# Four graph layers on one core: the R values of single edges picked two or three units ahead inside the products and summed one unit early, the spread of R moved there too, and the projection steps placed behind the products

## The chip, the core and the metric

The kernel runs on one core of one Trainium2 chip. The metric is the device time of one execution in microseconds (us): before the change the median of three runs is 2439.98 us (2439.79 to 2440.81). PE is the matrix engine (TensorE), PEld its weight loads, DVE the VectorE, ACT the ScalarE, POOL the GpSimd engine, SP the SyncE, which here only issues DMAs.

## The reference, cut to what matters

The input is x, 3327 rows of 512, and a 0/1 matrix adj of 3327 x 3327 whose rows and columns get sparser toward the end. Four layers follow one another, each on a layer-normed, clipped x and each added to x. Layers 0, 2 and 3 are graph attention with 8 heads of 64; layer 1 averages neighbours and multiplies.

```python
# attention (layer 2; 0 and 3 differ in names and in what follows)
Wh = jnp.einsum('nd,hdo->hno', x, W)
f1 = jnp.einsum('hno,ho->hn', Wh, a1)
f2 = jnp.einsum('hno,ho->hn', Wh, a2)
e = jax.nn.leaky_relu(f1[:, :, None] + f2[:, None, :], negative_slope=ALPHA)
e = jnp.where(adj[None, :, :] > 0, e, NEG_INF)
attention = jax.nn.softmax(e, axis=-1)
h_prime = jnp.einsum('hnm,hmo->hno', attention, Wh)
out = jax.nn.elu(h_prime)
...
h = jnp.maximum(_layernorm(x, axis=-1), 0.0)
x = x + _L2_gnn_ref(h, adj, L2_gnn_W, L2_gnn_a1, L2_gnn_a2)
```

Layer 0 puts a batch normalization and a relu after the product in place of the elu.

## The kernel before, in words

The program first makes, in the stretch up to about 352 us, lists of the neighbours of each group of 64 target rows (a group is `g`, 52 of them, two to a block of 128), and the projection of layer 0. Then it takes the sparse path, `sparse`; a dense path, `general`, is in the program but not run here.

One attention layer is one call of `attend` (L1319). The exponential of a leaky relu of a sum is written as a maximum of two products, so that a weight is max(R of the target, T of the source), times a factor of the source that is already inside the table's rows. R stands in `r_dram` and, as three bf16 parts whose sum is R, in `r3`; T and the projected values stand in a row of `table`.

The source rows of a group are cut into units (L1328). A *slot unit* holds up to 2 blocks (SLOTS) of 128 source rows with dense masks; a *unit of single edges* holds up to 3 (UNIT). There are 85 slot units and 90 units of single edges in a layer; most groups have one slot unit and then one or two units of single edges.

- A slot unit: `spread` (L1345) copies R of the group's 64 targets to all partitions with one product (L1350) into the bank `r_bc`. DVE takes the maximum with T (L1531, into the PSUM tile `mx`) and multiplies by the mask (L1535, `wgt`). PE multiplies the rows by it (L1564), 16 products a row (32 matmul records of the profile for two rows).
- A unit of single edges: each row belongs to one target. `pick` (L1470, product L1479) fetches its R by multiplying the transposed one-hot matrix `edges` with the three parts `r3`, into the PSUM tile `r_of`. DVE sums the three parts (L1517), takes the maximum with T (L1518), and scales the row (L1521, `vw`). PE adds it into its target with the one-hot matrix `ones_of` (L1553). `w_of`, the sum, lies in the PSUM tile of `mx`.
- In layer 0 alone the one-hot matrices are made on the way: DVE takes the bits (L1422), ACT makes masks of them (`masks`, L1439 to L1444), PE transposes them (`turned`, L1454), and ACT copies them to `edges` and out to `edges_dram` (`kept`, L1466). Layers 2 and 3 hold all `edges` in SBUF; layer 2 reads them back from `edges_dram` in five parts in its first five units (L1508).
- `load` (L1405) issues the fetches of a unit's rows three units ahead, from SP (contiguous rows) and POOL (gathers, L1314). `fetch` (L1339) loads R for the spread, two groups ahead.
- `later` (L1399) makes one step of each open `ending` (L1353: ACT copies the accumulator `facc` out, L1383, DVE takes reciprocals, L1387, ACT scales, L1393, then the layer's finish), and one of the work that goes beside the layer: in layer 0 the products and sums for layer 1 and for the batch normalization (`beside`, L1625; the sums L1675 and L1679), in layer 2 the projection for layer 3 (`Following.tick`, L841, with `norm`, L895, and `rest`, L960: p_ps L964, p_sd L972, p_wh L985, p_tr L999).

The order on PE, DVE and ACT is the order in which the code issues the work (L1336); semaphores are put in for the dependencies. PSUM tiles r_of, r_bc and mx have one buffer, the accumulator has two. For unit i the loop (L1503) issues: `load(i + 3)`; DVE's work of unit i, for single edges with the reduction L1517 first; `early(i)` (masks, then kept); `pick(i + 1)`; a spread for the next group if unit i-1 was the last slot unit; `later`; the next group's fetch; the products of unit i; and `turned`. `lead` (L1486) says how many units ahead the masks of a unit are made: 3 for single edges in layer 0, 2 in the others, 1 for slot units. `due(i)` lists the units whose turn it is.

Of the kernel before, what the change touches and what calls it, by code (L numbers as in the profile page):

```python
# [23 lines left out]
F32 = mybir.dt.float32  # L24
# [9 lines left out]
ALU = mybir.AluOpType  # L34
# [5 lines left out]
P = 128  # L40
H = 8
# [10 lines left out]
GB = 64  # L52
# [755 lines left out]
class Following:  # L808
# [468 lines left out]
def sparse(ctx: ExitStack, tc: tile.TileContext, t: dict, out: bass.AP, WA, ls, cs, idx, rdeg, first):  # L1277
# [41 lines left out]
    def attend(layer, table, r_dram, r3, finish, tick=lambda: None, home=None, beside=None, edges=None):  # L1319
# [14 lines left out]
        with tc.tile_pool(name=f"fatt{layer}", bufs=2) as ap, tc.tile_pool(  # L1334
            name=f"facc_ps{layer}", bufs=2, space=PSUM
        ) as aps, tc.manual_schedule(engines={ET.PE, ET.DVE, ET.Activation}):  # L1336
            loaded, ones_of, st_of, found, rrs, rbs, accs, ends, over = {}, {}, {}, {}, {}, {}, {}, [], []

            def fetch(j):  # L1339
                if j < len(groups):  # L1340
# [114 lines left out]

            def kept(i):

                if i < len(units) and units[i][2]:
                    _, g, _, rows, s0, _, _, _ = units[i]
                    u, n = g % PG, len(rows)  # L1460
                    mine = slice(u * GB, (u + 1) * GB)
                    if layer:
                        st_of[i] = edges[mine, s0 : s0 + n, :]
                        return
                    to = ap.tile([P, UNIT, P], BF16, name="edges", tag="edges", bufs=3)
                    nc.scalar.copy(to[mine, :n, :], st_of[i][mine, :n, :])  # L1466
                    nc.sync.dma_start(edges_dram[mine, s0 : s0 + n, :], to[mine, :n, :])
                    st_of[i] = to[mine, :n, :]

            def pick(i):  # L1470

                if i < len(units) and units[i][2]:
                    _, g, _, rows, s0, _, _, _ = units[i]
                    b, u = divmod(g, PG)
                    mine = slice(u * GB, (u + 1) * GB)
                    st = st_of.pop(i)
                    re = found[i] = aps.tile([P, UNIT, 3 * H], F32, name="r_of", tag="r_of", bufs=1)
                    for k in range(len(rows)):
                        nc.tensor.matmul(re[:, k, :], st[:, k, :], r3[mine, b, :], start=True, stop=True)  # L1479

            for j in range(2):
                fetch(j)
            spread(0)
            for i in range(AHEAD):
                load(i)
            lead = [(3 if layer == 0 else 2) if u[2] else 1 for u in units]  # L1486

            def due(i):

                return [k for k in range(max(i + 1, 0), i + 4) if k < len(units) and k - lead[k] == i]  # L1490
# [12 lines left out]
            for i, (j, g, e, rows, s0, begins, stops, last_slots) in enumerate(units):  # L1503
                n, m0 = len(rows), rows[0][0]
                gt = loaded.pop(i).bitcast(F32)
                T = gt[:, :n, H * (F + 1) : ROW]
                load(i + AHEAD)
                if layer == 2 and i < EPARTS:  # L1508
                    for u in range(PG):
                        mine = slice(u * GB, (u + 1) * GB)  # L1510
                        cut = slice(i * ls.used[u] // EPARTS, (i + 1) * ls.used[u] // EPARTS)
                        nc.sync.dma_start(edges[mine, cut, :], edges_dram[mine, cut, :])
                if e:
                    re = found.pop(i)
                    mx = aps.tile([P, SLOTS, H, GB], F32, name="w_of", tag="mx", bufs=1)
                    w = mx[:, 0, :UNIT, :H]
                    nc.vector.tensor_reduce(w[:, :n], re[:, :n].rearrange("p k (t h) -> p k h t", h=H), AX.X, ALU.add)  # L1517
# [3 lines left out]
                    nc.vector.tensor_tensor(  # L1521
                        vw[:, :n],
                        gt[:, :n, : H * (F + 1)].rearrange("p k (h x) -> p k h x", x=F + 1),
                        w[:, :n].unsqueeze(3).to_broadcast(full),
                        ALU.mult,
                    )
                else:
                    mk = mask[:, m0 : m0 + n, :]
                    full = [P, n, H, GB]
                    mx = aps.tile([P, SLOTS, H, GB], F32, name="mx", tag="mx", bufs=1)  # L1530
                    nc.vector.tensor_tensor(  # L1531
                        mx[:, :n], rbs[j].unsqueeze(1).to_broadcast(full), T.unsqueeze(3).to_broadcast(full), ALU.max
                    )
                    wt = ap.tile([P, SLOTS, H, GB], F32, name="wgt", tag="wgt", bufs=2 if layer == 0 else 3)
                    nc.vector.tensor_tensor(wt[:, :n], mx[:, :n], mk.unsqueeze(2).to_broadcast(full), ALU.mult)  # L1535
# [12 lines left out]
                for k in range(n):  # L1548
                    f, l = begins and k == 0, stops and k == n - 1
                    if e:  # L1550
                        by = vw[:, k].rearrange("p (q v) x -> p v q x", v=PG)
                        for v in range(PG):
                            nc.tensor.matmul(  # L1553
                                accs[g][v * GB : (v + 1) * GB, :sw].rearrange("p (q x) -> p q x", x=F + 1),
                                ones_of[i][:, k, :],
                                by[:, v],
                                start=f,
                                stop=l,
                            )
                        continue  # L1560
                    for q in range(hq):
                        for v in range(PG):
                            h = q * PG + v
                            nc.tensor.matmul(  # L1564
                                accs[g][v * GB : (v + 1) * GB, q * (F + 1) : (q + 1) * (F + 1)],
                                wt[:, k, h, :],
                                gt[:, k, h * (F + 1) : (h + 1) * (F + 1)],
                                start=(f and q == 0),
                                stop=(l and q == hq - 1),
                            )  # L1570
# [384 lines left out]
```

## Time and profile before

The profiled execution took 2678.83 us, the median of the runs 2439.98 us.

| What | Before |
|---|---|
| profiled execution, whole time | 2678.83 us |
| its span, first to last instruction | 2677.0 us |
| mean granted PE clock | 0.818 |
| lists and projection of layer 0 | 0 to about 352 us |
| attention of layer 0 | about 352 to 919 us |
| batch normalization, own part of layer 1 | about 919 to 1057 us |
| neighbours of layer 1, projection of layer 2 | about 1057 to 1517 us |
| attention of layer 2 | about 1552 to 2160 us |
| attention of layer 3 | about 2160 to 2660 us |

How to read it: a busy time is the union of an engine's instructions. A group of instructions has a line of the kernel, its count, its mean and the idle time of its engine just before it, with what ended that wait. A line "PE facc L1553 <- DVE vw L1521: 55.0, 48, 4.8" of the table of waits says that PE idled 55.0 us in 48 places, 4.8 at most, before products of L1553 until a DVE instruction of L1521 signalled. "issue" is idle time for which no semaphore is seen. Matmul ends are modelled[...].

### The profile page before, as it was taken

The page shows a single profiled execution, that of the slowest core. Times are in us where ns is not written, and L with a number is a line of the kernel's source. Part 1 is how long each engine was busy: PE and PEld are TensorE (multiplying, and loading weights), DVE is VectorE, ACT ScalarE, POOL GpSimd, SP SyncE. Part 2 cuts the span into 40 slices and gives each one's busy share as a digit, 9 for nine tenths or more (in the row PEclk, how much of TensorE's full clock was granted, in tenths as well). Part 3 has the DMA queues.
Part 4 walks back from the last instruction along what each step waited for, and adds up shares of the span by engine and source line. Part 5 has one row for each costly group of instructions (what it writes and reads, how often), then busy time and mean ns, then how long its engine had stood idle before and what let it go on. Part 6 is the DMA issues. An engine that isn't in the chain of part 4 may idle for free. (4 is left out here: it accounts for less than half of the span.)

```text
span 2677.0 us, 42990 instructions
## 1 busy us (share of the span) xinstructions
PE 1997.4 (75%) x14899; PEld 1129.0 (42%) x14899; DVE 1702.2 (64%) x3061; ACT 1113.8 (42%) x4149; POOL 1161.1 (43%) x1227
## 2 busy tenths in 40 slices
PE   6987157877777688879889847788788766767675
PEld 4644024545444344323333335454444444444442
DVE  5457856676667692124344557777667657788785
ACT  4555003344555542223233203667676702344443
POOL 1000034556655301666656245554445235666562
PEclk8788578988888899889999957889878866776676
DMA  7674068787777483778778587777667367887783
GB/s 278 237 269 172 7 226 273 241 254 213 220 219 234 131 292 129 259 239 266 249 234 274 161 259 221 210 229 210 203 187 217 104 212 224 233 242 237 223 248 94
DMA packets 213726, 577.60 MB, mean 216 GB/s; under 512 B 37838, under 2 KB 44076, under 8 KB 210174
## 3 DMA queue, kind: packets, MB, share of 16 engines
q0 software_dynamic: 93504, 328.25, 40.6%
q1 hardware_dynamic: 119998, 246.53, 27.6%
q8 instruction: 120, 1.97, 0.3%
q14 instruction: 104, 0.85, 0.1%
HBM read 511.41 MB, written 63.25 MB: 215 GB/s over the span
## 5 line engine op out<-in xcount | busy, mean ns | idle before, releaser
L1314 POOL DMA_INDIRECT rows_e<-table,idx x654 | 626.8, 958 | 395.4 <-issue 167.5
L1553 PE MATMUL facc<-vw,ones_of 128*64 128x260 f32 x2616 | 491.8, 496 | 101.9 <-DVE vw L1521 55.0
L1564 PE MATMUL facc<-rows_s,wgt 128*64 128x65 f32 x7200 | 353.7, 253 | 192.8 <-issue 117.4
L1564 PEld LDWEIGHTS facc<-rows_s,wgt 128*64 128x64 f32 x7200 | 305.7, 164 | 271.2 <-issue 166.7
L1314 POOL DMA_INDIRECT z_rows<-h_dram,idx x291 | 277.8, 955 | 301.9 <-issue 172.4
L1521 DVE TENSOR_TENSOR vw<-rows_e,w_of 128x1040 f32<-128x1040 f32 (+1 forms) x270 | 395.6, 1465 | 9.3
L1314 POOL DMA_INDIRECT rows_s<-table,idx x219 | 209.2, 955 | 418.0 <-PE r_of L1479 187.3
L1553 PEld LDWEIGHTS facc<-vw,ones_of 128*64 128x64 f32 x2616 | 236.5, 170 | 304.4 <-issue 193.2
L1531 DVE TENSOR_TENSOR mx<-r_bc,rows_s 128x1024 f32<-128x1024 f32 (+1 forms) x255 | 280.6, 1100 | 77.6 <-PE facc L1553 17.9
L1393 ACT ACTIVATE fhp<-sums,rd 64x64 f32<-64x64 f32 x816 | 215.5, 334 | 250.4 <-DVE rd L1387 199.6
L1535 DVE TENSOR_TENSOR wgt<-mx,mask 128x1024 f32<-128x1024 f32 (+1 forms) x255 | 280.3, 1099 | 50.5 <-PE facc L1564 24.2
L1517 DVE TENSOR_REDUCE w_of<-r_of 128x16 f32<-128x48 f32 (+1 forms) x270 | 60.7, 225 | 237.5 <-PE r_of L1479 103.5
L1839 PE MATMUL sage_acc<-z_rows,z_mask 128*64 128x512 f32 x736 | 189.0, 622 | 5.9 <-DMA z_rows<-h_dram 5.3
L1218 POOL DMA_DIRECT2D list_b<-shift x8 | 4.0, 514 | 322.2 <-DVE shift L1179 322.2
L1823 ACT CAST z_mask<-mask 128x128 f32<-128x128 uint8 (+1 forms) x201 | 52.0, 284 | 195.0 <-PE sage_acc L1839 85.2
L1792 DVE TENSOR_TENSOR s_o<-n_ps,bn_y 128x512 f32<-128x512 f32 x26 | 18.0, 692 | 173.6 <-PE n_ps L1787 105.0
L1383 ACT COPY sums<-facc 128x260 f32<-128x260 f32 x153 | 56.9, 372 | 164.8 <-PE facc L1553 116.3
L1444 ACT ACTIVATE mask<-on 128x128 uint8<-128x128 uint16 (+1 forms) x85 | 25.2, 296 | 240.9 <-DVE on L1422 199.7
L741 PE MATMUL wh_ps<-fWt,hT 128*128 128x512 f32 x208 | 122.2, 742 | 0.0
L1787 PE MATMUL n_ps<-fWx,aT 128*128 128x512 f32 x208 | 99.8, 624 | 20.4 <-issue 16.3
L926 PE MATMUL p_wh<-fWt,hT 128*128 128x512 f32 x208 | 104.0, 647 | 13.2 <-ACT hT L921 11.1
L1393 ACT ACTIVATE bn_y<-sums,rd 64x64 f32<-64x64 f32 x408 | 107.7, 334 | 3.1 <-DVE rd L1387 1.5
(260 smaller groups left out, 3038.3 us busy)
## 6 DMA issues: line engine op xcount, KB each, us to landing
adj_i<-in_adj SPq DMA_DIRECT2D x26, 1664.0 KB
rows_s<-table SPq DMA_DIRECT2D x46, 528.0 KB
table<-v_row SPq DMA_DIRECT2D x78, 264.0 KB
rows_s<-table SPq DMA_DIRECT2D x62, 264.0 KB
rows_s<-table SPq DMA_DIRECT2D x23, 632.0 KB
fin_x<-fx SPq DMA_DIRECT2D x52, 256.0 KB
z_rows<-h_dram SPq DMA_DIRECT2D x23, 512.0 KB
rows_e<-table,idx POOLq DMA_INDIRECT x654
```

The costliest lines, as they stand in the source:

```text
L741: nc.tensor.matmul(wh, hT[:, kc, :], self.Wt[:, kc, :], start=(kc == 0), stop=(kc == KC - 1))
L926: nc.tensor.matmul(wh, hT[:, kc, :], self.Wt[:, kc, :], start=(kc == 0), stop=(kc == KC - 1))
L1314: nc.gpsimd.indirect_dma_start(out=dst, out_offset=None, in_=src[:, :], in_offset=bass.IndirectOffsetOnAxis(ap=idx[:, k : k + 1], axis=0))
L1393: nc.scalar.mul(hp[o0 : o0 + GB, h * F : (h + 1) * F], sm[mine, q, 0:F], rd[mine, q, :])
L1517: nc.vector.tensor_reduce(w[:, :n], re[:, :n].rearrange("p k (t h) -> p k h t", h=H), AX.X, ALU.add)
L1521: nc.vector.tensor_tensor(vw[:, :n], gt[:, :n, : H * (F + 1)].rearrange("p k (h x) -> p k h x", x=F + 1), w[:, :n].unsqueeze(3).to_broadca ...
L1531: nc.vector.tensor_tensor(mx[:, :n], rbs[j].unsqueeze(1).to_broadcast(full), T.unsqueeze(3).to_broadcast(full), ALU.max)
L1535: nc.vector.tensor_tensor(wt[:, :n], mx[:, :n], mk.unsqueeze(2).to_broadcast(full), ALU.mult)
L1553: nc.tensor.matmul(accs[g][v * GB : (v + 1) * GB, :sw].rearrange("p (q x) -> p q x", x=F + 1), ones_of[i][:, k, :], by[:, v], start=f, stop=l,
L1564: nc.tensor.matmul(accs[g][v * GB : (v + 1) * GB, q * (F + 1) : (q + 1) * (F + 1)], wt[:, k, h, :], gt[:, k, h * (F + 1) : (h + 1) * (F + 1)],
L1787: nc.tensor.matmul(ps, aT[:, kc, :], Wx[:, 1, kc, :], start=(kc == 0), stop=(kc == KC - 1))
L1839: nc.tensor.matmul(acc[u * GB : (u + 1) * GB, :], m, z, start=f, stop=l)
```

## The change

For single edges, the pick of unit i+2 (layer 0) or i+3 (layers 2 and 3) is issued inside the products of unit i, after the products of its first row, or after all of them where the unit has one row (`others`). The spread for the next group goes there too, in the last slot unit itself. `r_of` keeps one buffer in layer 0 and gets two in the others. The reduction of unit i+1 (`summed`) is issued at the end of DVE's work of unit i. `later` comes after the products and the transposes. In `early`, kept copies come ahead of the masks. The five loads of edges in layer 2 come a unit earlier, the first ahead of the loop. `norm` yields once more between its ACT sums and the reciprocal square root on DVE. On each engine the number of instructions of each kind stays the same; of the projection of layer 3, four score products (L972) move from the loop to the stretch after it.

```diff
@@ norm
         step = rsqrt(nc, pp, cs, st[:, 2:3], 1.0 / D)
         yield
+        yield
         y = step()
@@ attend
-            loaded, ones_of, st_of, found, rrs, rbs, accs, ends, over = {}, {}, {}, {}, {}, {}, {}, [], []
+            loaded, ones_of, st_of, found, w_of, rrs, rbs, accs, ends, over = {}, {}, {}, {}, {}, {}, {}, {}, [], []
+            ahead = 2 if layer == 0 else 3
@@ kept
-                if i < len(units) and units[i][2]:
+                if layer == 0 and i < len(units) and units[i][2]:
...
-                    if layer:
-                        st_of[i] = edges[mine, s0 : s0 + n, :]
-                        return
@@ pick
-                    st = st_of.pop(i)
-                    re = found[i] = aps.tile([P, UNIT, 3 * H], F32, name="r_of", tag="r_of", bufs=1)
+                    st = st_of.pop(i) if layer == 0 else edges[mine, s0 : s0 + len(rows), :]
+                    re = found[i] = aps.tile([P, UNIT, 3 * H], F32, name="r_of", tag="r_of", bufs=ahead - 1)
...
+            def summed(i):
+
+                if i < len(units) and units[i][2]:
+                    n, re = len(units[i][3]), found.pop(i)
+                    mx = aps.tile([P, SLOTS, H, GB], F32, name="w_of", tag="mx", bufs=1)
+                    w = w_of[i] = mx[:, 0, :UNIT, :H]
+                    nc.vector.tensor_reduce(w[:, :n], re[:, :n].rearrange("p k (t h) -> p k h t", h=H), AX.X, ALU.add)
...
-            lead = [(3 if layer == 0 else 2) if u[2] else 1 for u in units]
+            lead = [(ahead + 1 if layer == 0 else 2) if u[2] else 1 for u in units]
...
             def early(i):
+                for k in due(i - 1):
+                    kept(k)
                 for k in due(i):
                     masks(k, bits(k))
-                for k in due(i - 1):
-                    kept(k)
-
-            for i in range(-3, 0):
+
+            def parts(i):
...
+            parts(0)
+            for i in range(-1 - ahead, 0):
                 early(i)
+                if i == -1:
+                    summed(0)
+                if i + ahead >= 0:
+                    pick(i + ahead)
@@ the loop over units
                 load(i + AHEAD)
...
+                parts(i + 1)
                 if e:
-                    re = found.pop(i)
-                    mx = aps.tile([P, SLOTS, H, GB], F32, name="w_of", tag="mx", bufs=1)
-                    w = mx[:, 0, :UNIT, :H]
-                    nc.vector.tensor_reduce(w[:, :n], re[:, :n].rearrange("p k (t h) -> p k h t", h=H), AX.X, ALU.add)
+                    w = w_of.pop(i)
...
+                summed(i + 1)
                 early(i)
-                if i == 0:
-                    pick(0)
-                pick(i + 1)
-                if i and units[i - 1][7]:
-                    spread(units[i - 1][0] + 1)
-                later()
                 if begins:
...
+                def others():
+                    pick(i + ahead)
+                    if last_slots:
+                        spread(j + 1)
+
                 for k in range(n):
+                    if k == 1:
+                        others()
...
+                if n == 1:
+                    others()
                 ones_of.pop(i, None)
                 for k in due(i):
                     turned(k)
+                later()
                 if stops:
                     ends.append(ending(g))
```

More of the change, by code (lines that the diff above doesn't have):

```diff
@@ L1485, in attend @@
                 load(i)
-            lead = [(3 if layer == 0 else 2) if u[2] else 1 for u in units]
+            lead = [(ahead + 1 if layer == 0 else 2) if u[2] else 1 for u in units]
             def due(i):
-                return [k for k in range(max(i + 1, 0), i + 4) if k < len(units) and k - lead[k] == i]
+                return [k for k in range(max(i + 1, 0), i + ahead + 2) if k < len(units) and k - lead[k] == i]
             def early(i):
+                for k in due(i - 1):
+                    kept(k)
                 for k in due(i):
                     masks(k, bits(k))
-                for k in due(i - 1):
-                    kept(k)
-            for i in range(-3, 0):
+            def parts(i):
+                if layer == 2 and i < EPARTS:
+                    for u in range(PG):
+                        mine = slice(u * GB, (u + 1) * GB)
+                        cut = slice(i * ls.used[u] // EPARTS, (i + 1) * ls.used[u] // EPARTS)
+                        nc.sync.dma_start(edges[mine, cut, :], edges_dram[mine, cut, :])
+            parts(0)
+            for i in range(-1 - ahead, 0):
                 early(i)
+                if i == -1:
+                    summed(0)
+                if i + ahead >= 0:
+                    pick(i + ahead)
                 for k in due(i):
@@ L1507, in attend @@
                 load(i + AHEAD)
[L1508 to L1512, printed above, removed]
+                parts(i + 1)
                 if e:
-                    re = found.pop(i)
-                    mx = aps.tile([P, SLOTS, H, GB], F32, name="w_of", tag="mx", bufs=1)
-                    w = mx[:, 0, :UNIT, :H]
-                    nc.vector.tensor_reduce(w[:, :n], re[:, :n].rearrange("p k (t h) -> p k h t", h=H), AX.X, ALU.add)
+                    w = w_of.pop(i)
                     nc.vector.tensor_tensor(w[:, :n], w[:, :n], T, ALU.max)
```

## The prediction

> **What bounds the kernel now.** I read the page's totals first, then a table of busy time by stage, then what the reduction of R waits for, then what TensorE (PE) waits for, and last a short timeline.
>
> ```profile
> span 2677.0 us, 42990 instructions
> ...
> PE 1997.4 (75%) x14899; PEld 1129.0 (42%) x14899; DVE 1702.2 (64%) x3061; ACT 1113.8 (42%) x4149; POOL 1161.1 (43%) x1227
> ```
>
> No engine is full. The three attention stages are 352 to 919, 1552 to 2160 and 2160 to 2660 us:
>
> ```profile
> core 0: us, PE busy (x) PEld busy (x) DVE busy (x) ACT busy (x) POOL busy (x), PEclk, DMA share, GB/s
> 352.00:919.00 567.00, 431.19 (x4154) 269.05 (x4155) 395.76 (x669) 255.79 (x849) 307.32 (x314) 0.86 0.75 234
> ...
> 1552.00:2160.00 608.00, 470.14 (x4087) 283.58 (x4087) 417.37 (x739) 351.76 (x1420) 273.14 (x286) 0.80 0.66 199
> 2160.00:2660.00 500.00, 345.69 (x3542) 222.34 (x3542) 391.76 (x544) 176.72 (x599) 279.67 (x291) 0.70 0.75 227
> ```
>
> In layers 0 and 2 PE leads VectorE (DVE) slightly, in layer 3 DVE leads, and neither passes 79% of its stage: they wait for each other. What DVE waits for at the first step of a unit of single edges, the reduction on L1517 (the first column is us, the second is times):
>
> ```profile
>   PE r_of L1479: 103.5, 61
>   PE facc L1564: 57.8, 27
>   remote: 31.4, 12
>   PE facc L1553: 17.6, 11
> ```
>
> With the small rest this is 237.5 us, in the groups by stage 119.3, 62.9 and 55.2. The reduction needs only the pick (L1479), so all of it is lateness of the pick; where another PE line is named, the pick's own signal came while PE was already further on. In return PE waits for DVE:
>
> ```profile
> PE facc L1553 <- DVE vw L1521: 55.0, 48, 4.8
> PE facc L1564 <- DVE wgt L1535: 51.2, 34, 7.2
> ...
> PE facc L1553 <- DVE rd L1387: 19.4, 15, 2.2
> ```
>
> One passage of layer 2 (start, length, engine):
>
> ```profile
> 1703.48 0.23 PE L1479 MATMUL r_of<-r_three,edges 64*128 64x24 bf16 x3
> ...
> 1703.65 5.40 PE L985 MATMUL p_wh<-fWt,hT 128*128 128x512 f32 x8
> ...
> 1708.98 1.15 PE L1564 MATMUL facc<-rows_s,wgt 128*64 128x65 f32 x32
> ...
> 1710.06 0.23 PE L1479 MATMUL r_of<-r_three,edges 64*128 64x24 bf16 x3
> ...
> 1710.34 0.24 DVE L1517 TENSOR_REDUCE w_of<-r_of 128x24 f32<-128x72 f32 x1 [1.72 <-PE r_of L1479]
> ```
>
> The weights of the slot unit were ready at 1703.0, yet its products start at 1708.98, behind a projection; the next pick stands behind those products, and DVE idles 1.72 us until it comes.
>
> **What the Trainium skill says.** "TensorE: Matmul & The Clock Gate", Part 1, gives PE a half and a full clock, chosen by recent activity. This trace agrees: mean clock 0.86, 0.80 and 0.70, and a product of L1553 averages 464 ns in layer 0 and 553 in layer 3. A denser PE may thus gain twice. The same page, Part 3, says that matmuls keep program order and only weight loads are pulled ahead; the passage above agrees, since nothing passed the 5.40 us block. "Perfetto Trace Analysis", section on the per-instruction lifecycle, says that waiting for a semaphore lies outside the reported window. The trace agrees: a pick starts at 1716.65 in 0.23 us, its reduction only at 1720.39. "PSUM — Partial Sum Buffer", Specifications, gives 8 banks of 2 KiB; layer 2 then holds 2 accumulators, 2 for mx, 1 r_bc, 2 picks and 1 projection tile, all 8. No run shows that limit yet.
>
> **The change part by part.** Instruction counts on every engine are equal before and after; only order and one buffer change.
>
> *Pick and reduction.* The pick of unit i+1 stood after the products of i-1. Now it stands after the first row of the products of i-1 in layer 0 (2 ahead), of i-2 in the others (3 ahead, two buffers), and its reduction runs at the end of unit i. The 237.5 us before L1517 should shrink to some 30. That is not the gain: DVE then meets the next late thing, and PE keeps its work. I bound each stage from both sides.
>
> Layer 0: PE idles 14.2 us before L1553 and 41.5 before L1564, of which 2.2 and 28.4 are "issue", pauses that no wait explains. The rest, 25.1, is what earlier weights can give. I take 20. The background sums (L1675, L1679) idle 16.3 and 21.4 waiting for ScalarE (ACT); moved behind products, they give ACT one more unit's products of time; I take half, 19.
> Layer 2: before L1553 and L1564 25.7 + 66.5, less 4.7 + 36.8 of "issue", is 50.7; take 36. Steps moved behind products, p_tr waits 11.3 us for DVE and p_ps idles 11.5: half would be 11, but partly they are the same time; take 6.
> Layer 3: 62.0 + 84.8, less 9.9 + 52.2, is 84.7 on PE's side. DVE's side is narrower: 391.8 busy plus its idle before L1531 and L1535 (33.7 and 12.6), plus about 10 elsewhere, is 448 of 500, so 52 at most; take 42.
>
> *Spread (L1350).* 51 a layer, about 0.58 us each, moved from after a unit's products to inside them. DVE idles 5.8, 30.5 and 33.7 us before L1531, part of it for this (11.7 us named). The gain is in the sums above. Price of failing cover: in the middle of products the r_bc bank must be read out; the last L1531 of that group precedes the very products, so it is free.
>
> *Kept copies (L1466), layer 0.* The 90 copies average 0.41 us. The pick now comes half a unit's products earlier, right behind the transposes of the unit before, one background step and one row. If ACT is inside eight scalings (8 x 334 ns = 2.7 us), the pick waits, and the second row's products wait behind it. Before, picks waited for it 4.4 us in all (their weight loads 5.3). Bounds: zero, if those steps hide 0.41 us, to 51 x 2.7 = 138. Putting the copy ahead of the masks helps. I take 0.3 us for each of 51 groups: 15 lost.
>
> *Later steps behind products, and the second yield.* On each engine they stay in the same cyclic order; only PE's part moves past the products, and SP's row store, fin_x loads and r_dram writes past the r_two load. SP's cover is that r_two is fetched two groups ahead; without it the price is like the 3.9 us seen once before r_bc. Cost nothing. The second yield parts the inverse square root from its ACT sums: DVE waited 22.0 us for ln_j in layer 2. That is inside layer 2's 36. The edge loads of layer 2 come one unit earlier: nothing, since five parts go out in the first units, while the first pick comes in the eighth. The moved order leaves more of one block for the end of layer 2: its four score products go from p_sd to mx. The end took from 2130 to 2160 for three blocks, 10 us each, but only one block's middle steps move: bounds 0 and 10, take 4 lost.
>
> Sum: 20 + 19 - 15 = 24, 42, 42, less 4: 104 us, so the profiled execution goes from 2678.8 (span 2677.0) to about 2575. The median of the runs shown is 2439.98, 239 us shorter. PE's unexplained pauses inside products (117.4 + 16.8 us of "issue"), in steps of about 0.7 us, are probably part of that difference, and 107 of the 237.5 us at L1517 were ended by another PE line or unnamed, as in such pauses. So I carry over 0.62 of the gain, near the 55% that remain: 64 us, or **2375**.
>
> **The rivals.**
> 1. *The wait moves.* DVE gets its reduction early and then stands at L1531 for r_bc, at the two or three weight buffers, or at rows; PE, already busy 431 and 470 us, cannot use the lead. For it: idle before L1531 is 70 us and PE is the longer engine in two stages. Against it: the spread moves forward too. A third of the gain, 35 x 0.62 = 22: 2418.
> 2. *ACT becomes the gate, slower than before.* An accumulator is freed by L1383 on ACT, two groups later. ACT serves in order, and the steps it serves before (hT, eight L994 scalings of 328 ns, 2.6 us) now get their PE operands only behind the products, a unit later, while L1383 keeps its deadline; in layer 0 the kept copy is squeezed likewise. If each of 51 groups in layer 2 pays 2.6 and in layer 0 1.0 us more on PE: 184 lost against 104 won, +80 x 0.62 = 50: 2490. It decides from a mean of about 1 us per group (104/102). For it: ACT is busy 352 of 608. Against: products wait for L1383 by name under 10 us now.
> 3. *Full decoupling.* DVE stays fed and PE denser at a higher clock: the stages end at DVE's busy time plus 8%, 427, 451 and 423 instead of 567, 608 and 500: 374 us less on paper, but PE's 431 and 470 forbid most of the first two unless its clock rises. I take rather more than half of it, 215, x 0.62 = 133: 2307.
> That it doesn't do what it says is excluded: the order of instructions shows picks inside products in all three layers.
>
> **How the numbers follow.** Forecast 0.52 (its own range 2350 to 2400), wait moves 0.20, ACT gate 0.14, full decoupling 0.14. What this kernel's measurement can tell from no change is about 0.2%, 5 us. Of "wait moves", 0.05 falls within it. Faster 0.81, same 0.05, slower 0.14. The range reaches from most of case 3 to the start of case 2, with the copies' and drain's bounds: 2300 to 2450.
>
> **What would show it.** Right: idle before the reduction under 60 us in all, PE's waits for vw and wgt under 50, stages near 543, 566 and 458, the background sums' waits halved, clock in layer 3 not below 0.70. Wrong: the same idle before L1531's and L1535's successors; or picks waiting for edges, and products waiting for sums, for more than 100 us together; or an end of layer 2 longer by over 10 us. Carrying the gain over to unprofiled runs is my weakest step: a gain of 100 there, or of 30, would break that step alone.

## The result, and the profile after

The changed kernel takes 2428.31 us (median of 20 runs, 2411.37 to 2444.31), the kernel before 2439.89 (20 runs, 2430.72 to 2453.55): ratio 0.9952, 95% interval 0.9931 to 0.9972. It is faster by 11.6 us, 0.5%, where I forecast 64. All runs of this study fall at one of two levels, at which the kernel before takes about 2440 or 2664 to 2690 us, and versions timed side by side shared one; the profile from which I forecast is of the longer level (2678.83), the result of the shorter.

The changed kernel's page, span and engines, from an execution of 2440.86 us:

```profile
span 2439.1 us, 43174 instructions
...
PE 1925.1 (79%) x14899; PEld 1060.8 (43%) x14899; DVE 1705.3 (70%) x3061; ACT 1111.4 (46%) x4149; POOL 1161.0 (48%) x1227
```

PE has the same 14899 matmuls as before. To compare stages I need a profile of the kernel before that agrees with its median; that is the run "before, third time" below (span 2442.9). Its busy time by stage, for the attention of layer 0, the neighbours of layer 1, and the attention of layers 2 and 3 (columns as in the prediction: after the busy times of the five engines come PE's mean clock, the DMA share and GB/s):

```profile
357.00:865.00 508.00, 393.18 (x4153) 244.28 (x4154) 395.98 (x666) 255.61 (x846) 302.82 (x311) 0.92 0.79 257
1003.00:1399.00 396.00, 384.86 (x1338) 143.85 (x1334) 167.85 (x356) 134.03 (x640) 275.37 (x289) 0.98 0.86 285
1434.00:1965.00 531.00, 424.73 (x4036) 261.45 (x4036) 404.70 (x701) 339.13 (x1363) 273.04 (x286) 0.83 0.73 226
1999.00:2425.00 426.00, 302.25 (x3541) 199.61 (x3541) 388.59 (x540) 176.36 (x597) 276.14 (x287) 0.79 0.82 263
```

And the changed kernel's:

```profile
350.00:846.00 496.00, 396.60 (x4154) 241.21 (x4155) 396.03 (x667) 254.45 (x845) 302.78 (x311) 0.91 0.80 264
984.00:1385.00 401.00, 387.56 (x1339) 144.24 (x1338) 168.35 (x356) 134.35 (x641) 276.12 (x289) 0.98 0.85 281
1420.00:1964.00 544.00, 457.63 (x4027) 267.57 (x4028) 407.59 (x702) 336.42 (x1355) 274.15 (x286) 0.79 0.72 220
2003.00:2420.00 417.00, 312.83 (x3541) 193.41 (x3541) 386.28 (x538) 174.31 (x590) 276.11 (x287) 0.79 0.83 268
```

Layer 0 gains 12 us and layer 3 gains 9, but layer 2 loses 13. In layer 2 PE has nearly the same count of products in 457.6 us of busy time in place of 424.7, at a clock of 0.79 in place of 0.83. Each stage is read from one execution, and the changed kernel's lies 12.5 us above its median of 2428.31: in a median run some of layer 2's loss may not be there.

The wait before the reduction is gone, as planned. Before (third time), then after, in the tables of what DVE waited for:

```profile
DVE w_of L1517 <- PE r_of L1479: 86.6, 61, 5.4
DVE w_of L1517 <- PE facc L1553: 0.8, 1, 0.8
```

```profile
DVE w_of L1486 <- PE r_of L1478: 4.7, 7, 1.3
DVE w_of L1486 <- PE facc L1579: 0.5, 1, 0.5
```

With the rest of the group, DVE's idle time before the reduction went from 96.6 us to 31.2. The wait to win was thus 97 us, not 237.5. PE's waits for DVE did not fall with it. Before, then after:

```profile
PE facc L1564 <- DVE wgt L1535: 102.7, 76, 6.5
PE facc L1553 <- DVE vw L1521: 60.1, 85, 2.9
```

```profile
PE facc L1579 <- DVE wgt L1548: 109.2, 82, 8.0
PE facc L1568 <- DVE vw L1534: 58.8, 78, 2.6
```

What DVE stands at instead shows in layer 2 of the changed kernel, in the same table cut to 1420 to 1964 us:

```profile
DVE r_three L803 <- ACT r_three L799: 30.6, 11, 5.2
DVE s_col L983 <- ACT s_col L980: 28.9, 17, 4.5
DVE fin_x L1622 <- ACT fin_x L1620: 16.1, 13, 3.0
...
DVE rd L1389 <- ACT sums L1385: 13.3, 7, 3.2
DVE r_half L797 <- ACT r_half L793: 5.2, 5, 1.6
DVE w_of L1486 <- PE r_of L1478: 1.9, 2, 1.3
```

Waits that name ACT (with one small row more) are 96 us of layer 2 (544 us); in the kernel before they were 48, beside 36 for the pick. All these are steps of `later`, which the change moved behind the products.

### The profile page after: what moved, and what is told of

Read it like the earlier page. It is cut to its first block, busy times and chain, and to the rows that moved or that the text cites. A ratio compares the mean times of both kernels' runs of the same rounds, so it can differ in the third digit from the quotient of the medians.

```text
span 2439.1 us, 43174 instructions
## 1 busy us (share of the span) xinstructions
PE 1925.1 (79%) x14899; PEld 1060.8 (43%) x14899; DVE 1705.3 (70%) x3061; ACT 1111.4 (46%) x4149; POOL 1161.0 (48%) x1227
## 5 line engine op out<-in xcount | busy, mean ns | idle before, releaser
L1568 PE MATMUL facc<-vw,ones_of 128*64 128x260 f32 x2616 | 472.3, 469 | 78.1 <-DVE vw L1534 58.8
L1579 PEld LDWEIGHTS facc<-rows_s,wgt 128*64 128x64 f32 x7200 | 300.3, 161 | 284.5 <-DVE wgt L1548 133.7
L1568 PEld LDWEIGHTS facc<-vw,ones_of 128*64 128x64 f32 x2616 | 191.7, 158 | 217.2 <-issue 91.2
L1857 PEld LDWEIGHTS sage_acc<-z_rows,z_mask 128*64 128x64 f32 x736 | 51.4, 138 | 117.3 <-issue 95.7
L1779 PE MATMUL s_ps<-fWx,hT 128*128 128x512 f32 x208 | 93.3, 602 | 6.2 <-ACT hT L1776 6.2
```

What stands on the lines that cost most here:

```text
L1568: nc.tensor.matmul(accs[g][v * GB : (v + 1) * GB, :sw].rearrange("p (q x) -> p q x", x=F + 1), ones_of[i][:, k, :], by[:, v], start=f, stop=l,
L1579: nc.tensor.matmul(accs[g][v * GB : (v + 1) * GB, q * (F + 1) : (q + 1) * (F + 1)], wt[:, k, h, :], gt[:, k, h * (F + 1) : (h + 1) * (F + 1)],
L1779: nc.tensor.matmul(ps, hT[:, kc, :], Wx[:, 0, kc, :], start=(kc == 0), stop=(kc == KC - 1))
L1857: nc.tensor.matmul(acc[u * GB : (u + 1) * GB, :], m, z, start=f, stop=l)
```

## The experiments

**With the kernel before at 2664 to 2690 us: this kernel twice more, the parts alone, and the whole change.** The first four stand beside a median of 2689.5 us for the kernel before, the next four beside 2663.7.

> The kernel before, profiled once more. Theory 1 (the profile shown of before was of an unusually slow execution, 239 us above the median, by pauses of PE in stages the change does not touch too): its span comes out near 2440 us, the neighbours' stage of layer 1 near 400 instead of 460 us, and the idle time before the reduction of R (L1517) at 100 to 150 us instead of 237. Theory 2 (profiling lengthens this kernel, and the changed one less): span again near 2680 and L1517 again near 237.

Measured: 2696.2 us in its one run, with 253.6 us of idle time before L1517. Plain runs beside it took as long (2689.5), so the profiling does not make the difference.

Picks and early reduction alone (the change without the moved spread, the moved `later` and the second yield):

> The picks and the early reduction alone; spread, later steps and the inverse square root as before. Theory A (picks gain, the later steps behind the products take it back): ratio 0.97 to 0.985. Theory B (an undisturbed kernel before waits little for the reduction, and what it waits is only moved to the next late thing): ratio 0.99 to 1.00, idle before the reduction under 20 us, idle before other DVE lines up by most of what it was.

Measured: 2698.8, ratio 1.0047 (1.0028 to 1.0066).

The moved steps alone:

```diff
-                later()
                 if begins:
...
                 for k in due(i):
                     turned(k)
+                later()
```

> The later steps behind the products and transposes alone; picks, spread and the inverse square root as before. Theory A: slower, ratio 1.01 to 1.03, with DVE waiting for ACT in layer 2 (s_col, r_three, fin_x) as the changed kernel does, some 80 us. Theory B: within 0.5% of before either way.

Measured: 2701.4, ratio 1.0049 (1.0030 to 1.0067).

The spread inside the products alone:

```diff
-                if i and units[i - 1][7]:
-                    spread(units[i - 1][0] + 1)
...
                 for k in range(n):
+                    if k == 1 and last_slots:
+                        spread(j + 1)
```

> The spread of R inside the last slot unit's products alone, all else as before. Both theories: within 0.4% of before, as DVE's idle time before L1531 has other ends than r_bc; a gain over 0.5% would say that r_bc was a gate of its own.

Measured: 2693.0, ratio 1.0016 (0.9997 to 1.0035). No part gains here.

The whole change:

> The whole change again. On the chip of the first four runs the kernel before takes 2690 us instead of 2440, with pauses of PE of about 0.7 us, and there the single parts alone gave 1.0047 (picks), 1.0049 (later steps) and 1.0016 (spread). Theory 1 (the parts work only together: an early pick needs an early spread and products that are not behind the later steps): below 1.00 on either kind of chip, by 0.5% to 2%. Theory 2 (the parts add up): 1.011 on a chip of the slow kind; on a chip of the fast kind 0.995 as measured.

Measured: 2676.8 against 2663.7, ratio 1.0041 (1.0013 to 1.0068). So where the kernel before runs as in the profile from which I worked, the change loses 13 us; the sum said 104 won.

> The kernel before, profiled once more. On a chip of the fast kind its span should be near 2440 us, with the neighbours' stage of layer 1 near 400 us, and the idle time before the reduction L1517 says what there was to win: theory 1 says 100 us or more, moved elsewhere by the change; theory 3 (the profile used for the forecast came from a chip of the slow kind, and on a fast one DVE hardly waits for picks) says under 60. On the slow kind: 2690 and 250 again.

Measured: 2666.5 in one run, with 226.3 us before L1517.

The whole change with `later` back ahead of the products, then with the spread back after them:

> The change with the later steps put back ahead of the products. Theory 1 (parts need each other): slower than the whole change by 0.5% or more. Theory A (the later steps behind the products cost DVE its waits for s_col, r_three and fin_x in layer 2): faster than the whole change by 0.5% or more, with those waits down from 76 us to under 40.

Measured: 2663.2, ratio 1.0008 (0.9988 to 1.0029), 13.6 us below the whole change: without the moved steps the loss is gone.

> The change with the spread put back to the start of the unit after the last slot unit. Theory 1: slower than the whole change by 0.5% or more, with DVE idle before the maximum for slot units (mx) up from 28 us to 80 or more, as in the run of the picks alone, where it stood at 136. If the spread is no gate, within 0.3% of the whole change.

Measured: 2679.2, ratio 1.0067 (1.0031 to 1.0103). The interval overlaps that of the whole change: what the moved spread is worth is not told.

**With the kernel before at 2440 us.** It had 2440.74, 2441.92 and 2442.87 us beside the runs from here on.

The kernel before, third time:

> The kernel before once more, on a chip drawn anew, for its trace. Two chips so far gave 2664 and 2690 us for it, while the result's twenty runs gave 2440. If this chip is of the faster sort (2440), my theory of two sorts of chips says that the idle time ahead of the reduction (L1517) is far below the 237 us of the profile shown, 100 to 150 us, and that the neighbours' stage that the change does not touch lasts near 401 us as in the changed kernel's profile. The rival, that the changed kernel alone runs without the pauses, says 237 us and 460 us. On a chip of the slower sort it repeats 237 us and tells nothing new.

Measured: 2444.66 in one run, with the waits shown above: 97 us of idle time before L1517 in the groups, and 396 us for the neighbours' stage. The kernel before shows the difference of 240 us by itself; the change does not make it. The expectations put it down to the chip; that is not shown, for the chip with number 11 on record ran the kernel before in 2689.5 and in 2441.9 us. What makes it stays unknown.

The change with `later` back ahead of the products, once more:

```diff
                 early(i)
+                later()
...
                     turned(k)
-                later()
```

> The whole change with the projection steps put back ahead of the products. On the slower sort of chip the whole change cost 0.4% and this version nothing (1.0008). If the steps behind products are what eats the gain on every sort of chip, this is 0.990 or less of the kernel before on the faster sort (the whole change there 0.9952). If on the faster sort they cost nothing, it is 0.995. On a chip of the slower sort both say 1.000 to 1.003.

Measured: 2387.91, ratio 0.9785 (0.9760 to 0.9810). This is 53 us below the kernel before: the moved steps eat 41 of them. Layer 2 lasts 480 us, with a shorter busy time of PE at a higher clock, and its waits for ACT are few. The stage, and the table of what DVE waited for there:

```profile
1427.00:1907.00 480.00, 405.49 (x4028) 239.60 (x4025) 403.71 (x701) 336.66 (x1356) 272.87 (x285) 0.90 0.80 249
```

```profile
DVE r_three L803 <- ACT r_three L799: 17.4, 8, 4.7
...
DVE w_of L1486 <- PE r_of L1478: 6.0, 7, 2.3
DVE r_half L797 <- ACT r_half L793: 3.5, 4, 1.5
DVE fin_x L1622 <- ACT fin_x L1620: 3.2, 3, 1.7
DVE rd L1389 <- ACT sums L1385: 1.5, 1, 1.5
...
DVE s_col L983 <- ACT s_col L980: 0.2, 1, 0.2
```

The same, with layer 0's pick after a unit's last product:

```diff
-                    if k == 1:
+                    if k == 1 and layer:
                         others()
...
-                if n == 1:
+                if n == 1 or not layer:
                     others()
```

> As the one before, and the picks of layer 0 come after a unit's last product in place of after its first row's, so that the kept copy of the edges has the whole unit to arrive. In the changed kernel TensorE waited 51 us for that copy in layer 0. If those waits sit on the path, this is 20 to 50 us faster than the version beside it; if the reduction is then late again by as much (theory of waits that only move), it is within 5 us of it, with the idle time ahead of the reduction in layer 0 larger and that for the kept edges smaller.

Measured: 2392.36, ratio 0.9800 (0.9774 to 0.9826), not told apart from the one beside it. The expectation gives 51 us for PE's wait for the kept edges; the traces of the changed kernel name 15.2 us of it beside the result and 39.1 in the run of 2676.8. With the steps ahead of the products it is 2.0 us in the version beside this one and 1.8 here, so this run could gain nothing.

`later` ahead of the products in layer 2 alone:

```diff
                 early(i)
+                if layer == 2:
+                    later()
...
-                later()
+                if layer != 2:
+                    later()
```

> The whole change, with the projection steps ahead of the products in layer 2 alone, and behind them in layers 0 and 3. On the faster sort of chip the change's stages lasted 495, 544 and 416 us, with all steps put back 508, 480 and 417, the kernel before 508, 531 and 426. If each stage keeps its own effect, this one has 495, 480 and 416: some 13 us below the version with all steps put back, 2375 us, 0.973 of the kernel before. If the background sums' waits in layer 0 only move, it is 2388, 0.978. On the slower sort, 0.995 to 1.000.

Measured: 2382.14, ratio 0.9747 (0.9720 to 0.9773). The stages are 498, 486 and 417 us: layer 0 keeps its gain, layer 2 is back:

```profile
1418.00:1904.00 486.00, 415.67 (x4028) 246.06 (x4024) 403.89 (x700) 336.75 (x1355) 273.04 (x286) 0.88 0.79 246
```

So the price of the moved steps is in layer 2, 46 us in the medians (2428.3 less 2382.1) and 58 in the profiled stages (544 less 486). The profiled executions lie 56 us apart (2440.86 and 2384.43), which is the greater part of that mismatch.

The whole change, with one step of the projection a unit in place of two:

```diff
-        for _ in range(min(2, len(self.ready))):
+        for _ in range(min(1, len(self.ready))):
```

> The whole change as it is (steps behind products everywhere), but in layer 2 one step of a block's projection is taken behind each unit, not two. Theory: behind the products TensorE's part of a step comes a unit's products later, ScalarE, which serves in order, stands at it, and VectorE then stands at the step after it; with one step a unit each has a whole unit more, so the waits for s_col, r_three and fin_x (76 us together in layer 2 of the changed kernel) fall below 30, and layer 2 returns from 544 to 480 to 500 us: 2365 to 2390 in all. Rival, that the place behind the products costs by TensorE's order alone (the blocks of 0.7 us products then stand between two units' products wherever ScalarE is): layer 2 stays at 530 to 545, 2415 to 2430. An end of layer 2 that is longer by up to 20 us, since steps pile up, is possible in both.

Measured: 2419.22, ratio 0.9901 (0.9876 to 0.9925), layer 2 at 527 us. That is near what the rival said (530 to 545); DVE's wait for s_col stayed at 25.5 us. I had overlooked that one step a unit leaves DVE's clamp (L983) one unit behind PE's product (L973), as it was.

Both of these together:

> As the first of these (steps ahead of the products in layer 2), with one step a unit in layer 2. Theory: with the steps ahead of the products the waits for s_col, r_three and fin_x were only 28 us, so 0 to 20 us better than the first. Rival: no better, or worse by the longer end of layer 2.

Measured: 2367.41, ratio 0.9685 (0.9659 to 0.9711): the fastest version here, 61 us below the changed kernel and 74.5 below the kernel before beside it. It is 15 us below the one before it, within the 0 to 20 of its theory.

The kernel before with the moved steps alone, once more:

> The kernel before, with only the projection steps put behind the products. On the faster sort of chip: if their price of 64 us in layer 2 and their gain of 13 in layer 0 stand by themselves, 2490 us, 1.02 of the kernel before. If they cost only where the early picks have already taken VectorE's waiting away (the two waits overlap), 2430 to 2450, 0.995 to 1.004. On the slower sort it was 1.0049.

Measured: 2474.99, ratio 1.0138 (1.0114 to 1.0163). The moved steps cost without the early picks too, 33 us in layer 2 (564 for 531), so they do not only take the place of the waits that the picks removed; the first of the two cases is right in sign, with 33 us in all in place of 50.

The whole change with more room between PE's part and DVE's step:

```diff
         nc.scalar.copy(sf, sd[:, :H])
         yield True
+        yield True
+        yield True
...
         nc.sync.dma_start(self.table[c * P : (c + 1) * P, :ROW], row.bitcast(I32))
         yield True
+        yield True
+        yield True
```

> The whole change as it is (steps behind products everywhere), with two empty steps in layer 2's projection after the copy of s_col, and two after the row's store, so that VectorE's clamp of s_col and its r_half come two units after TensorE's product, not one. Theory: the price of 64 us in layer 2 is VectorE's lead, since a step of VectorE that needs TensorE's part through ScalarE finds that part a unit later than before. The waits for s_col (28.9), r_half (5.2) and part of those for r_three (30.6) should go, those for fin_x and rd (29) stay: layer 2 from 544 to 505 to 520 us, 2385 to 2405 in all. Rival (VectorE then waits elsewhere for the same products, or TensorE is the limit there): 535 or more, 2415 to 2435.

Measured: 2457.76, ratio 1.0082 (1.0050 to 1.0113), layer 2 at 562 us. The theory was wrong; the rival's 535 or more holds for the layer, though the whole lies above its 2415 to 2435. DVE's waits in layer 2:

```profile
DVE r_three L803 <- ACT r_three L799: 35.8, 13, 5.7
DVE rd L1393 <- ACT sums L1389: 25.4, 19, 4.0
DVE fin_x L1626 <- ACT fin_x L1624: 21.0, 7, 4.6
...
DVE s_col L985 <- ACT s_col L980: 0.8, 1, 0.8
```

The wait for s_col went, from 28.9 to 0.8, as the longer distance should do it, yet all waits for ACT together are 95 us as before (96). They only changed places. So the short distance of these two steps is not by itself the cause.

What the other parts are worth, picks and early reduction alone, and these with the spread but without the second yield:

> The earlier picks and reduction alone: spread, projection steps and the norm's steps as in the kernel before. The version with all but the moved projection steps gained 52 us (0.9785). If picks and reduction carry it, 2388 to 2400, 0.978 to 0.984; if the spread and the second yield carry half, 2410 to 2420. The forecast put 22 us of waiting for ln_j, which the second yield should remove, inside layer 2's gain.

Measured: 2435.77, ratio 0.9982 (0.9964 to 1.0001).

```diff
         yield
-        yield
         y = step()
```

(on the change with `later` put back)

> The change with the projection steps put back, and without the second yield in the norm. If that yield is worth the 23 us that VectorE waited for the row sums in the kernel before, 2410; if the wait only moves, 2388 to 2395.

Measured: 2437.46, ratio 0.9985 (0.9964 to 1.0007). Both expectations that gave the picks the gain fall. Picks, early reduction and spread together bring at most 9 us, and their intervals reach to no gain; the second yield on top of them brings the other 50 (2437.46 less 2387.91), twice what I expected of it here. The wait that it removes, in layer 2 of the version without it:

```profile
DVE rs_h L774 <- ACT ln_j L902: 24.7, 11, 5.7
```

With it, layer 2 has no such wait. The second yield was not tried without the picks, so it is not shown whether it needs them.

**These versions side by side.** Stages in us; the last four columns are of layer 2: PE's clock, its busy time, DVE's waits that name ACT (summed from the table of waits), and DVE's waits for the pick. The ratio is of the medians, all else of one execution; layer 0, whose code the versions "and steps moved in 0, 3" and "and one step a unit" share, differs by 6 us between them, so single stages are no finer than that.

| Version | Ratio | Layers 0 / 2 / 3 | Clock | PE busy | for ACT | for pick |
|---|---|---|---|---|---|---|
| before, third time | 1 | 508 / 531 / 426 | 0.83 | 424.7 | 48 | 36 |
| before, steps moved | 1.0138 | 504 / 564 / 425 | 0.80 | 441.3 | 80 | 39 |
| picks alone | 0.9982 | 509 / 538 / 417 | 0.81 | 445.5 | 57 | 17 |
| picks and spread | 0.9985 | 508 / 529 / 416 | 0.81 | 443.6 | 52 | 21 |
| and second yield | 0.9785 | 508 / 480 / 417 | 0.90 | 405.5 | 26 | 6 |
| and steps moved in 0, 3 | 0.9747 | 498 / 486 / 417 | 0.88 | 415.7 | 25 | 9 |
| and one step a unit | 0.9685 | 504 / 478 / 416 | 0.88 | 409.9 | 14 | 10 |
| whole change | 0.9952 | 496 / 544 / 417 | 0.79 | 457.6 | 96 | 2 |
| whole, one step a unit | 0.9901 | 496 / 527 / 416 | 0.83 | 438.9 | 73 | 1 |
| whole, more room | 1.0082 | 499 / 562 / 416 | 0.79 | 460.1 | 95 | 10 |

## Why the prediction was wrong

The step that failed is this one: *"Later steps behind products, and the second yield. On each engine they stay in the same cyclic order; only PE's part moves past the products … Cost nothing."* The observation on the order is right, the price is not. The moved steps cost 46 us in the medians, all in layer 2: the version that puts them back there alone wins that much. Without that the change takes 2382, and the forecast said 2375; but that it comes so near is luck, as the other terms show.

How it costs shows in a passage of layer 2 of the changed kernel (start, length, engine):

```profile
1703.58 0.17 DVE L1389 RECIPROCAL rd<-sums 128x4 f32<-128x4 f32 x1
...
1703.93 1.78 DVE L1534 TENSOR_TENSOR vw<-rows_e,w_of 128x1560 f32<-128x1560 f32 x1
...
1704.49 0.84 PE L1579 MATMUL facc<-rows_s,wgt 128*64 128x65 f32 x16
...
1705.26 1.89 PE L973 MATMUL p_sd<-WA,hT 128*128 128x16 f32 x8
...
1707.19 0.19 ACT L977 ACTIVATE v_row<-p_sd 128x8 f32<-128x8 f32 x1 [4.32 <-PE p_sd L973]
...
1707.41 0.17 ACT L980 COPY s_col<-p_sd 128x8 f32<-128x8 f32 x1
1707.60 2.14 ACT L1395 ACTIVATE fhp<-sums,rd 64x64 f32<-64x64 f32 x8
1707.61 0.17 DVE L983 TENSOR_SCALAR s_col<-s_col 128x8 f32<-128x8 f32 x1 [1.90 <-ACT s_col L980]
1707.72 1.23 DVE L1544 TENSOR_TENSOR mx<-r_bc,rows_s 128x1024 f32<-128x1024 f32 x1
```

p_sd stands behind the slot products of 1704.49. ACT, whose next work needs it, stands 4.32 us, and DVE, whose next work needs ACT, stands 1.90 us. Only then does it begin the maximum for the next unit. The same trace has hT, which p_sd needs, complete at 1702.87, so ahead of those products p_sd could have started sooner. ACT waits longer for PE's projection results in all: in layer 2 of the changed kernel

```profile
ACT v_row L995 <- PE p_wh L986: 45.7, 16, 7.7
ACT hT L968 <- PE p_ps L965: 45.5, 21, 5.7
ACT v_row L977 <- PE p_sd L973: 37.0, 18, 4.6
```

against these with the steps put back:

```profile
ACT v_row L995 <- PE p_wh L986: 21.4, 13, 4.1
ACT hT L968 <- PE p_ps L965: 16.3, 17, 2.9
...
ACT v_row L977 <- PE p_sd L973: 11.1, 11, 1.4
```

"TensorE: Matmul & The Clock Gate", Part 1, of the Trainium skill calls ACT and DVE strict first-in-first-out queues. The passage agrees: the scaling of fhp had its reciprocal from DVE at 1703.75 (1703.58 and 0.17), yet it began only at 1707.60, behind the steps that read p_sd. So does the run with more room: with s_col's wait taken away, DVE's waits at rd and fin_x, which come from ACT too, were longer, 46 us in place of 29. That is rival 2's mechanism (ACT in order gets PE's operand a unit later), at another place than I put it: what waits for ACT is DVE's next step, not PE's products for the accumulator.

The larger part of the loss is not pauses but PE's pace. From "and second yield" to the whole change layer 2 grows by 64 us: PE's busy time by 52 (405.5 to 457.6), its pauses by 12 (75 to 86). The products are the same, and busy time times clock is nearly equal: 405.5 x 0.90 = 365, 457.6 x 0.79 = 362. The second yield shows the same: of the 49 us by which it shortens layer 2, 38 are PE's busy time (443.6 to 405.5, at 0.81 and 0.90). I wrote that a denser PE may gain twice, and then priced idle time alone. That the longer waits lower the clock is argued from the table, not shown: the clock is 0.88 to 0.90 in the three versions with 14 to 26 us of waits for ACT and 0.79 to 0.83 in all with 48 or more, but among the latter it follows them only in part (0.83 beside 73 us, 0.81 beside 52). No run changed the clock alone.

The other terms:

- *Bound, and idle before L1517 from 237.5 to some 30.* Direction right; 97 to 31 beside the result. The profile of 2678.83 us was the wrong base: of its 117.4 us of "issue" at L1564 10.6 are left in the third one of the kernel before, and of the waits at L1517 that named other PE lines 0.8, as I had suspected.
- *The factor 0.62.* The sum without what it grants the moved steps (19 in layer 0, 6 in layer 2) is 79, times 0.62 is 49; measured 53 without them. This agrees by accident: the picks, the early reduction and the spread, for which it stood, bring at most 9, and the second yield, which I held to be 22 us before the factor, brings 50.
- *Layer 0: 20 less 15 for the copies.* Times 0.62, 3; measured 0. The wait of picks for the copies was 15.2 us in the changed kernel. Copies ahead of the masks took away the 23.0 us that PE's transposes waited for the copies in the kernel before (third time), but then they waited 23.7 for the one-hot masks. *Background sums, 19:* times 0.62, 12; measured 10, from 508 to 498, and 4 to 12 over all versions with these steps moved. The sum is about right, though the waits did not halve but went, 35.0 us to 1.5 for both lines, and the stage kept less than half of that. The first line at PE, before and after:

```profile
L1675 PE MATMUL bsum_ps<-bn_d,fones 128*64 128x512 f32 (+1 forms) x52 | 31.9, 699 | 17.3 <-ACT bn_d L1685 17.2
```

```profile
L1693 PE MATMUL bsum_ps<-bn_d,fones 128*64 128x512 f32 (+1 forms) x52 | 29.4, 649 | 0.3 <-ACT bn_d L1703 0.3
```

- *Layer 2: 36.* Mis-sized twice. Picks and spread bring 2 us of stage (531 to 529): DVE's wait for the pick falls by 15, but PE's clock falls too, and its busy time grows by 19, of which the clock (0.83 to 0.81) accounts for about half. The second yield, which I held to be 22 of the 36, brings 49.
- *Layer 3: 42.* Times 0.62, 26; measured 9. DVE was busy 389 of 426 us before; the stage had little left.
- *Drain of layer 2: 4 lost.* From 34 us between the stages of layers 2 and 3 to 39: right in size. But the moved steps alone make it 36, and the version with the second yield and the steps put back 42: the yield, to which I gave no part in it, lengthens it.
- *Show-tests.* Idle before the reduction under 60: met. PE's waits for vw and wgt under 50: 168, missed. Yet they are 152 (97.0 and 54.8) in the version that gains 53 us, and 163 before, so this test does not tell failure from success. The signs of being wrong that I gave as numbers stayed out too: picks waited 15 us for edges and the accumulator's products 22 for sums, together far below 100, and the end of layer 2 grew by 5, not over 10. None of them looked at DVE's waits for ACT.

Open: why the second yield brings 49 us where the wait that it removes had 24.7, and why more room in the projection costs 18. Both shift all later steps of a block against the units, so what collides at ACT may decide; no run isolates that. `later` holds the steps of the open endings and those of the projection, and no run moved one without the other. Open too is why the change without the moved steps gains nothing beside a kernel before of 2663.7 us (1.0008).

## What to carry to other kernels

A chain that runs from one engine through a second, in-order one to a third is not free to move because each engine keeps its own order: count by how much of the first engine's work the producer moves back against the consumer, and who is queued behind the engine between. Price a pause of TensorE with its clock, since the same products took 405 or 458 us of busy time here. And take the base of a sum from a profile whose own time agrees with the median; here 240 us lay between them, and the change won 11.6 us beside a kernel before of 2440 and lost 13 beside one of 2664.

## What the runs showed of the hardware that I had not expected

One program gave two quite different profiles. In that of 2678.83 us PE pauses inside runs of slot products without a named wait; in the third one of the kernel before (2444.66) waits for DVE and ACT come first. The row of these products in both:

```profile
L1564 PE MATMUL facc<-rows_s,wgt 128*64 128x65 f32 x7200 | 353.7, 253 | 192.8 <-issue 117.4 <-DVE wgt L1535 51.2 <-ACT fhp L1393 12.5
```

```profile
L1564 PE MATMUL facc<-rows_s,wgt 128*64 128x65 f32 x7200 | 313.7, 246 | 157.0 <-DVE wgt L1535 102.7 <-ACT ones_of L1442 18.5 <-ACT sums L1383 14.7
```

From one such product to the start of the next, 0.55 to 0.9 us pass 65 times in the first and 6 times in the second. The cause stays unknown.

The clock records of the traces hold 1.0 and 0.5 only, and each but a trace's last lasts a whole multiple of 3.41 us. In layer 2 PE ran at half clock for 223 us of the changed kernel's 544, in 22 stretches, and for 98 of 480, in 15, with the steps put back. The same page of the skill, Part 1, ties the half clock in its table of states to an idle window of about 3.4 us, and further on tells of a kernel in which frequent short idle times between groups of products brought it too. These traces are nearer to the second: only two pauses of PE in either stage were 3.4 us long, and those of 1 us or more were 34 and 24. How many short pauses it takes is not told: the kernel before had 39 in layer 2 with 179 us at half clock.
